# One number read back by VectorE after every step of a four-way scan

## The chip, the cores and the metric

The kernel runs on one core of one Trainium2 chip. The metric is the device time of one execution in microseconds (us). The time before the change is 9154.29 us, the median of three runs (9152.1 to 9154.33).

## What is computed

The input is a float32 image stack of shape (4, 48, 256, 256). Four layers follow each other, each of the form `x = x + f(group_norm(x))`. Layer 0 is a channel attention, layer 1 a gated convolution. Layers 2 and 3, which the change concerns, are the same chain of four scans with different weights:

```
step(carry, inp) = inp + conv1d(carry, w, b)      # 5 taps, 48 channels to 48
down : over the rows, first to last               # input x
up   : over the rows of the result, last to first # the down weights again
right: over the columns, first to last            # the right weights
left : over the columns of that, last to first    # the left weights
```

Every step needs the whole result of the step before it. The four images are independent of each other.

## The kernel before

**Pairs and chains.** The images are worked on two at a time. A pair lies on 96 partitions (48 channels times two neighbouring positions of a row), so that one step of a scan is, for each image of the pair, three matrix products of a 96x96 weight with a 96x128 slice of the last state, summed in PSUM. `scans` (line 965) makes one generator per pair, `chain(pair)` (line 1015); every `yield` in it is one step. I call them chain 0 and chain 1. At the end of `scans` the two are woven: chain 0 takes `lead` = 992 steps alone, then both step in turn, and when chain 0 is through, chain 1 has its last steps alone (lines 1390 to 1404). Beside these last steps `to_rows(0)` rearranges chain 0's result, with copies on GpSimd (line 1383) and ScalarE (line 1385) into a tile `oo`, loaded from `oi`.

**One step** is `step(layer, way, inp, after)`, line 1037. The state lives in four buffers `carry` (`NC` = 4, line 1001) that are used in turn. For each of the two images i:

- TensorE: three matmuls of line 1045 into `ps` (the profile shows six instructions for them, each 96x96 with 96x128);
- VectorE: one addition `carry = ps + inp` (line 1049 for inputs that lie in blocks, line 1053 for plain ones);
- `after(new, b)`, called `keep`: ScalarE writes the new state with its bias to where it is stored (line 1127 down, 1168 up, 1187 for the last row, 1248 right), or, in the left scan, GpSimd adds it to the residual tile `stage` (line 1289) or into `done` (line 1293; this is the last scan of chain 1, the case `direct`).

The addition of step t+1 writes the buffer that was written at step t-3. So besides the sum in `ps` it waits for the `keep` of step t-3, which reads that buffer: for ScalarE in the first three scans, for GpSimd in the left one. In the right scan it also waits for its input: `fetch` (line 1221) copies a strided column out of a block to a plain tile `pre` on GpSimd (line 1225), three steps ahead of its use.

**Order of the work.** Each engine works through one queue in order. The order in the queues is not the order of the Python code: the framework's planner walks through the traced instructions and gives an engine an instruction when, by its own estimates of durations, its inputs are ready; of several that are ready the one that comes first in the code goes first. Line 1317, the `bn_stats` of the first of the two layers, shows it: the code has one of them after each step (`late.pop(0)()`, line 1300), while the trace has eight within four steps. The planner also writes all semaphore waits.

**Stages and transfers.** Down and up work in blocks of 32 rows (line 1117, 1145): down loads the next block (line 1120) and normalises it on ScalarE in place in four pieces (line 1123, `norm`, line 1104, 96x2048 elements each) during the second half of the present one. Right and left work in blocks of 16 columns (lines 1230, 1272) and load the next block at the first step of the present one (lines 1235, 1279, 1280). Stores leave at the ends of blocks (lines 1136, 1201, 1260, 1303, 1311). All of these transfers are issued from SyncE's queue.

Of the kernel before, what the change touches and what calls it, by code (L numbers as in the profile page):

```python
# [9 lines left out]
F32 = mybir.dt.float32  # L10
# [9 lines left out]
P = 96  # L20
# [5 lines left out]
NK = W // (2 * KC)  # L26
# [938 lines left out]
def scans(ctx, tc, xs, out, wts, biases, dram, k, coefs, lead, spare):  # L965
# [13 lines left out]
    nc = tc.nc  # L979
# [8 lines left out]
    wp = pool("c_w", 1)  # L988
# [10 lines left out]
    CB = 2 * KC  # L999
# [15 lines left out]
    def chain(pair):  # L1015
# [4 lines left out]
            nc.gpsimd.memset(c, 0.0)  # L1020
        last = wp.tile([P, 2, W // 2], F32, tag=f"last{pair}", name=f"last{pair}")
        at = [0]

        def slot(name):
            return take(pair, f"{name}{pair}")
# [43 lines left out]
        def load_rows(layer, n, ts, k0, k1):  # L1069

            for r in range(2):
                v = rows_view(ts[r])
                for q in range(2):
                    for b in range(2):
                        nc.sync.dma_start(
                            v[q * C : (q + 1) * C, b, k0:k1].rearrange("c k h w -> c k (h w)"),
                            xs[layer][pair][
                                r * C : (r + 1) * C, b, 2 * k0 + q : 2 * k1 - 1 + q : 2, n * NH : (n + 1) * NH, :
                            ].rearrange("c k h w -> c k (h w)"),
                        )  # L1080

        def layer_of(layer, first):
# [32 lines left out]
            for n in range(NT):  # L1115
                ahead_ = None
                for r in range(RT):
                    if r == 0 and n + 1 < NT:
                        ahead_ = [slot("dn"), slot("dn")]
                        load_rows(layer, n + 1, ahead_, 0, NK)  # L1120
                    if ahead_ and r >= RT // 2 and r % 4 == 0:
                        i = (r - RT // 2) // 4
                        norm(ahead_, i // 2, i % 2)
                    inp = row(now, r)

                    def keep(new, b):
                        nc.scalar.activation(inp[:, b], blocks(new[:, b]), AF.Identity, bias=bias[:, 0:1])  # L1127

                    if n == 0 and r == 0:
                        keep(inner(), slice(0, 2))  # L1130
                    else:
                        step(layer, 0, inp, keep)
                    yield
                if ahead_:
                    for r in range(2):
                        nc.sync.dma_start(D[n][r], now[r])
                    now = ahead_
# [4 lines left out]
            column = None  # L1142
            for n in reversed(range(NT)):
                ahead_ = None
                for r in reversed(range(RT)):
                    if r == RT - 1 and n > 0:
                        ahead_ = [slot("up"), slot("up")]
                        for i in range(2):
                            nc.sync.dma_start(ahead_[i], D[n - 1][i])
                    if n == 0 and r == RT // 4:  # L1150

                        column = slot("col")
                        v = cols_view(column)
                        for par in range(2):
                            for b in range(2):
                                h0 = NH + 1 - par
                                here = slice(par * C, (par + 1) * C)
                                nc.sync.dma_start(
                                    v[here, b, :, h0:, :].rearrange("c q h w -> c q (h w)"),
                                    U[here, b, 0:2, h0:, :].rearrange("c q h w -> c q (h w)"),  # L1160
                                )
                    i = n * RT + r + 1
                    if i == H:
                        continue
                    place = row(now, r)

                    def keep(new, b):
                        nc.scalar.activation(place[:, b], blocks(new[:, b]), AF.Identity, bias=bias[:, 1:2])  # L1168

                    if i == H - 1:  # L1170
                        keep(inner(), slice(0, 2))
                    else:
                        step(layer, 0, place, keep)
                    yield
                    if n == 0 and r < 2:

                        par, h0 = 1 - r, r
                        v = cols_view(column)
                        for q in range(2):
                            nc.sync.dma_start(  # L1180
                                v[par * C : (par + 1) * C, :, q, h0 : h0 + NH, :].rearrange("c b h w -> c b (h w)"),
                                rows_view(now[r])[q * C : (q + 1) * C, :, 0].rearrange("c b h w -> c b (h w)"),
                            )
                if n == 0:

                    def keep(new, b):
                        nc.scalar.activation(last[:, b], new[:, b], AF.Identity, bias=bias[:, 1:2])

                    step(layer, 0, blocks(last), keep)
                    yield  # L1190
                    for q in range(2):
                        nc.sync.dma_start(cols_view(column)[0:C, :, q, 0, :], last[q * C : (q + 1) * C, :, 0:KC])
                for r in range(2):
                    v = rows_view(now[r])
                    par = 1 - r
                    nh = NH - (r == 1 and n == NT - 1)
                    h0 = n * NH + r
                    for q in range(2):
                        for b in range(2):
                            nc.sync.dma_start(  # L1200
                                U[par * C : (par + 1) * C, b, q::2, h0 : h0 + nh, :].rearrange("c k h w -> c k (h w)"),
                                v[q * C : (q + 1) * C, b, :, :nh, :].rearrange("c k h w -> c k (h w)"),
                            )
                if n == 0:
                    for q in range(2):
                        for b in range(2):
                            nc.sync.dma_start(
                                U[0:C, b, q::2, 0, :],
                                last[q * C : (q + 1) * C, b].rearrange("c (k w) -> c k w", w=KC),
                            )  # L1210
                now = ahead_
# [7 lines left out]
            fetched = {}  # L1219

            def fetch(block, n, w):
# [3 lines left out]
                nc.gpsimd.tensor_copy(t, cols_view(block)[:, :, w % 2, :, w // 2])  # L1225
                fetched[g] = t

            for w in range(1, 3):
                fetch(column, 0, w)
            for n in range(NK):  # L1230
                ahead_ = None
                for w in range(CB):
                    if w == 0 and n + 1 < NK:
                        ahead_ = slot("col")
                        nc.sync.dma_start(by_batch(ahead_), block_of(U, n + 1))
                    if w == 0 and n + 1 == NK:
                        stage = slot("stage")
                        nc.sync.dma_start(by_batch(stage), block_of(x, n))
                    if w == 0:
                        lines = slot("lines")  # L1240
                    if w + 3 < CB:
                        fetch(column, n, w + 3)
                    elif ahead_ is not None:
                        fetch(ahead_, n + 1, w + 3 - CB)
                    line = lines_view(lines)[:, w]

                    def keep(new, b):
                        nc.scalar.activation(line[:, b], new[:, b], AF.Identity, bias=bias[:, 2:3])  # L1248

                    if n == 0 and w == 0:  # L1250

                        nc.vector.tensor_scalar(
                            advance(), cols_view(column)[:, :, 0, :, 0], bias[:, 1:2], None, ALU.subtract
                        )
                        keep(inner(), slice(0, 2))
                    else:
                        step(layer, 1, fetched.pop(n * CB + w), keep)
                    yield
                if ahead_ is not None:
                    nc.sync.dma_start(Rt[n], lines)  # L1260
                    column = ahead_
# [3 lines left out]
            if layer == 0:  # L1265
                stats = [wp.tile([P, NK * 4, 6], F32, tag=f"st{pair}{b}", name="st") for b in range(2)]
            following = None


            direct = layer == 1 and pair == NP - 1  # L1270
            done = None
            for n in reversed(range(NK)):
# [3 lines left out]
                for w in reversed(range(CB)):  # L1276
# [18 lines left out]
                    if n == NK - 1 and w == CB - 1:  # L1295
                        keep(inner(), slice(0, 2))
                    else:
                        step(layer, 2, line, keep)
                    if late:
                        late.pop(0)()  # L1300
                    yield
# [227 lines left out]
```

## Time and profile before

| what | value |
|---|---|
| median of the three runs | 9154.29 us |
| the profiled execution | 9152.88 us, of which the span from first to last instruction is 9151.1 us |
| TensorE busy | 8728.1 us, 95% of the span |
| VectorE busy | 3763.0 us, 41%, 10790 instructions |
| ScalarE busy | 3489.5 us, 38% |
| GpSimd busy | 2073.9 us, 23% |
| mean granted TensorE clock | 0.979 |
| first and last matmul of line 1045 | 3234.0 us, 9120.9 us |

A page of this profiler shows busy times by engine and by group of instructions, the idle time before each group and what ended it, and the chain of work that ended last. A row of a group gives line, engine, operation, output and inputs, shapes and count, then busy us and mean ns of one. "PE" is TensorE, "DVE" VectorE, "ACT" ScalarE, "POOL" GpSimd, "SP" SyncE. A "q" behind an engine's name means its sequencer: EVENT_SEMAPHORE is an instruction that only waits. The ends of matmuls are modelled, their starts are recorded.

From the recorded starts of the additions, and the order of the two chains in the program, the scans lie like this in the profiled execution (us from the start):

| chain, layer | down | up | right | left |
|---|---|---|---|---|
| 0, layer 2 | 3243 to 3859 | 3860 to 4202 | 4209 to 4578 | 4579 to 4954 |
| 0, layer 3 | 4987 to 5639 | 5642 to 6306 | 6314 to 6980 | 6985 to 7643 |
| 1, layer 2 | 3542 to 5518 | 5521 to 6188 | 6195 to 6859 | 6863 to 7530 |
| 1, layer 3 | 7567 to 7964 | 7964 to 8310 | 8323 to 8688 | 8689 to 9121 |

Until about 4936 us chain 0 is nearly alone (chain 1 has 63 additions of its own before 4900 us besides 21 at about 3550 us); from 4936 to 7643 us both run; after that chain 1 is alone.

### The profile page before, as it was taken

The numbers are of one execution on the slowest core, as the hardware profiler recorded it, in microseconds if no ns is written. First come the engines' busy times: TensorE is split into PE (matmuls) and PEld (weight loads), VectorE is DVE, ScalarE is ACT, GpSimd is POOL, SyncE is SP. The second block draws the span as 40 slices with busy tenths as digits, with TensorE's granted clock in tenths as the row PEclk, the third lists the DMA queues.
The fourth block names the chain that finished last, engine by engine and source line by source line (L and its number), as shares of the span: only waits on it lengthen the run. The fifth ranks groups of instructions, "written<-read, shape, count | busy, mean of one in ns | idle before, by whom it ended". The sixth has DMA issues, their size and how long they took to land.

```text
span 9151.1 us, 162340 instructions
## 1 busy us (share of the span) xinstructions
PE 8728.1 (95%) x62920; PEld 7283.8 (80%) x62920; DVE 3763.0 (41%) x10790; ACT 3489.5 (38%) x7033; POOL 2073.9 (23%) x3855
## 2 busy tenths in 40 slices
PE   6999999999999887999999999999999999999986
PEld 4777777433333346999999999999999999998986
DVE  3232010234555564444455444444445554343432
ACT  0001000123343356755502766665661006665500
POOL 0000000001111120002464000003446772003464
PEclk9999999999999988999999999999999999999998
DMA  7663323468788868665587773656556787888677
GB/s 149 133 132 87 73 63 72 95 138 175 173 182 181 174 156 178 130 141 138 142 218 172 146 159 92 153 130 169 145 161 186 218 220 158 180 183 203 172 153 146
DMA packets 1177350, 1390.61 MB, mean 152 GB/s; under 512 B 261072, under 2 KB 1103568, under 8 KB 1113600
## 3 DMA queue, kind: packets, MB, share of 16 engines
q1 hardware_dynamic: 1176480, 1379.90, 66.5%
q8 instruction: 493, 8.08, 0.4%
q14 instruction: 281, 2.30, 0.1%
q0 software_dynamic: 96, 0.33, 0.0%
HBM read 812.02 MB, written 509.61 MB: 144 GB/s over the span
## 4 chain that ended last, share of the span: by engine, by line
PE 89%; DMA 4%; DVE 3%; ACT 2%; issue 1%; SPq 1%; POOL 1%; DVEq 0%; POOLq 0%; ACTq 0%
PE ps L1045 58%; PE py L581 7%; PE acc L294 5%; PE acc L295 5%; PE acc L296 4%; PE py L590 4%; PE pt L276 1%; DMA stage<-x 1%; DMA tok<-x 1%; PE ph L698 1%; ACT x1n L541 1%; PE pout L868 1%; PE ptok L751 1%; DMA x<-y 1%; DMA sx<-in_x 1%
## 5 line engine op out<-in xcount | busy, mean ns | idle before, releaser
L1045 PE MATMUL ps<-carry,w 96*96 96x128 f32 x48960 | 5505.8, 275 | 135.9 <-DVE carry L1053 89.3
L1045 PEld LDWEIGHTS ps<-carry,w 96*96 96x96 f32 x48960 | 5456.1, 163 | 188.9 <-DVE carry L1053 100.5
L1225 POOL COPY pre<-col 96x256 f32<-96x256 f32 x1020 | 656.7, 645 | 2737.5 <-DMA col<-last 1948.3
L1248 ACT ACTIVATE lines<-carry,b 96x128 f32<-96x128 f32 (+1 forms) x2044 | 816.9, 402 | 623.6 <-DVE carry L1053 614.5
L1127 ACT ACTIVATE dn<-carry,b 96x128 f32<-96x128 f32 (+1 forms) x2044 | 770.5, 398 | 715.0 <-DVE carry L1049 712.1
L1049 DVE TENSOR_TENSOR carry<-ps,dn 96x128 f32<-96x128 f32 x2280 | 655.2, 288 | 892.9 <-PE ps L1045 803.3
L1053 DVE TENSOR_TENSOR carry<-ps,pre 96x128 f32<-96x128 f32 x2040 | 587.2, 288 | 796.8 <-PE ps L1045 544.0
L1168 ACT ACTIVATE up<-carry,b 96x128 f32<-96x128 f32 x1792 | 718.3, 402 | 481.6 <-DVE carry L1049 480.6
L1053 DVE TENSOR_TENSOR carry<-ps,lines 96x128 f32<-96x128 f32 x2040 | 577.0, 286 | 741.4 <-PE ps L1045 645.4
L1289 POOL TENSOR_TENSOR stage<-stage,carry 96x128 f32<-96x128 f32 (+1 forms) x1533 | 793.1, 521 | 312.3 <-DVE carry L1053 184.2
L1049 DVE TENSOR_TENSOR carry<-ps,up 96x128 f32<-96x128 f32 x1792 | 516.4, 288 | 678.3 <-PE ps L1045 668.9
L581 PE MATMUL py<-x1n,wy 128*96 128x512 f32 x1536 | 700.8, 605 | 30.2 <-ACT x1n L541 27.9
L294 PE MATMUL acc<-xt 128*96 128x288 f32 x2048 | 666.9, 409 | 0.0
L295 PE MATMUL acc<-xs,xt 128*96 128x288 f32 x2048 | 666.9, 407 | 0.0
L581 PEld LDWEIGHTS py<-x1n,wy 128*96 128x96 f32 x1536 | 244.0, 165 | 452.4 <-issue 435.0
L261 ACT ACTIVATE xn<-raw,coef 96x2048 f32<-96x2048 f32 x64 | 133.6, 2094 | 986.9 <-PE pt L276 819.8
L296 PE MATMUL acc<-xt,xs 128*96 128x192 f32 x2048 | 501.7, 327 | 0.0
L279 DVE COPY xt<-pt 128x384 f32<-128x384 f32 x256 | 136.6, 554 | 851.5 <-PE pt L276 650.6
L296 PEld LDWEIGHTS acc<-xt,xs 128*96 128x96 f32 x2048 | 332.2, 165 | 154.4 <-issue 1.5
L295 PEld LDWEIGHTS acc<-xs,xt 128*96 128x96 f32 x2048 | 332.1, 164 | 151.2 <-issue 2.4
L604 DVE TENSOR_TENSOR y<-py,t 96x512 f32<-96x512 f32 x256 | 171.4, 677 | 592.1 <-PE py L590 586.2
L590 PE MATMUL py<-x2n,wy 64*96 64x512 f32 x1536 | 363.0, 601 | 0.0
(179 smaller groups left out, 4843.4 us busy)
## 6 DMA issues: line engine op xcount, KB each, us to landing
stage<-x SPq DMA_DIRECT2D x64, 1536.0 KB
dn<-x SPq DMA_DIRECT2D x240, 384.0 KB
col<-U SPq DMA_DIRECT2D x60, 1536.0 KB
R<-lines SPq DMA_DIRECT2D x60, 1536.0 KB
lines<-R SPq DMA_DIRECT2D x60, 1536.0 KB
D<-dn SPq DMA_DIRECT2D x56, 1536.0 KB
up<-D SPq DMA_DIRECT2D x56, 1536.0 KB
U<-up SPq DMA_DIRECT2D x224, 384.0 KB
```

The source lines that it names most:

```text
L294: nc.tensor.matmul(acc[0], lhsT=xt[:, h + 2, :], rhs=xt[:, here, :], start=first, stop=last)
L295: nc.tensor.matmul(acc[1], lhsT=xt[:, h + 2, :], rhs=xs[:, here, :], start=first, stop=last)
L296: nc.tensor.matmul(acc[2], lhsT=xs[:, h + 2, :], rhs=xt[:, past, :], start=first, stop=last)
L581: nc.tensor.matmul(ps, lhsT=held["w"][0][:, dx], rhs=x1n[:, 2 * c : 2 * c + 2, dx : dx + W], start=dx == 0, stop=False)
L590: nc.tensor.matmul(held["ps"][q + 2 * s], lhsT=held["w"][1][here, dx], rhs=x2n[here, 2 * q : 2 * q + 2, dx : dx + W], start=False, stop=dx ...
L1045: nc.tensor.matmul(ps, lhsT=w_sb[layer][:, way, j, :], rhs=old[:, i, j : j + W // 2], start=j == 0, stop=j == 2)
L1049: nc.vector.tensor_add(new[:, i].rearrange("p (k w) -> p k w", w=KC), ps.rearrange("p (k w) -> p k w", w=KC), inp[:, i])
L1053: nc.vector.tensor_add(new[:, i], ps, inp[:, i])
L1127: nc.scalar.activation(inp[:, b], blocks(new[:, b]), AF.Identity, bias=bias[:, 0:1])
L1168: nc.scalar.activation(place[:, b], blocks(new[:, b]), AF.Identity, bias=bias[:, 1:2])
L1248: nc.scalar.activation(line[:, b], new[:, b], AF.Identity, bias=bias[:, 2:3])
L1289: nc.gpsimd.tensor_add(to[:, b], to[:, b], new[:, b])
```

## The change

A tile `seen` of one number per partition and a list `kept` are added to each chain. After every step, `look` notes the place that this step's `keep` writes for the second image (one column of it). From the fourth call on, VectorE reads the place noted three steps before into `seen`: a copy of 96x1 elements; in the right scan an addition of that number and one number of the next step's fetched column. The list is emptied at the start of every block of 32 rows in down and up, and at the start of right and of left. The additions, `keep` and all else stay as they are; a chain issues 968 readings per layer.

```diff
+        seen = wp.tile([P, 1], F32, tag=f"seen{pair}", name="seen")
+        kept = []
+
+        def look(place, fetched=None):
+            kept.append(place)
+            if len(kept) > 3:
+                if fetched is None:
+                    nc.vector.tensor_copy(seen, kept.pop(0))
+                else:
+                    nc.vector.tensor_add(seen, kept.pop(0), fetched)
...
                         step(layer, 0, inp, keep)
+                    look(inp[:, 1, 0, 0:1])
                     yield
...
                         step(layer, 0, place, keep)
+                    look(place[:, 1, 0, 0:1])
                     yield
...
                         step(layer, 1, fetched.pop(n * CB + w), keep)
+                    if n + 1 < NK or w + 1 < CB:
+                        look(line[:, 1, 0:1], fetched[n * CB + w + 1][:, 1, 0:1])
                     yield
...
                         step(layer, 2, line, keep)
+                    if direct:
+                        look(done[1].rearrange("p (h w) -> p h w", w=2 * CB)[:, 0, n % 2 * CB + w : n % 2 * CB + w + 1])
+                    else:
+                        look(to[:, 1, 0:1])
                     if late:
                         late.pop(0)()
                     yield
```

`kept.clear()` stands at `r == 0` in down, at the start of each block in up, and once ahead of right and of left.

More of the change, by code (lines that the diff above doesn't have):

```diff
@@ L1120, in layer_of @@
                         load_rows(layer, n + 1, ahead_, 0, NK)
+                    if r == 0:
+                        kept.clear()
                     if ahead_ and r >= RT // 2 and r % 4 == 0:
@@ L1144, in layer_of @@
                 ahead_ = None
+                kept.clear()
                 for r in reversed(range(RT)):
@@ L1226, in fetch @@
                 fetched[g] = t
+            kept.clear()
             for w in range(1, 3):
@@ L1267, in layer_of @@
             following = None
+            kept.clear()
             direct = layer == 1 and pair == NP - 1
```

## Prediction

> **What bounds the kernel now.** I read the page's busy times first, then its row of line 1045, then a table of five windows, then the source view of line 1053 and single additions in the timeline.
>
> ```profile
> PE 8728.1 (95%) x62920; PEld 7283.8 (80%) x62920; DVE 3763.0 (41%) x10790; ACT 3489.5 (38%) x7033; POOL 2073.9 (23%) x3855
> ...
> L1045 PE MATMUL ps<-carry,w 96*96 96x128 f32 x48960 | 5505.8, 275 | 135.9 <-DVE carry L1053 89.3
> ```
>
> TensorE is nearly always busy, but its ends are modelled: a short hold of each group does not show as idle. Matmuls counted per window show it:
>
> ```profile
> 3900.00:4150.00 250.00, 250.00 (x2232) 249.72 (x2231) 107.09 (x372) 149.39 (x372) 0.00 (x0) 1.00 0.62 145
> 4350.00:4500.00 150.00, 150.00 (x1312) 146.03 (x1311) 62.91 (x219) 87.59 (x218) 70.27 (x109) 1.00 0.50 136
> 7000.00:7250.00 250.00, 250.00 (x2286) 250.00 (x2285) 132.10 (x429) 0.00 (x0) 196.03 (x381) 1.00 0.78 217
> ```
>
> All three are 100% busy at full clock. With both chains (last row) a matmul comes every 109.3 ns, so 12 of them, one step of a chain, take 1.311 us: TensorE's own rate. Chain 0 alone in up (first row) has 112.0 ns, in right (second) 114.3 ns. The recorded starts of additions give the same: 1.344 us a step alone in down, up and left, 1.3755 us in right. There the loop addition, matmuls, addition is longer than TensorE's work.
>
> ```profile
> L1053 DVEq EVENT_SEMAPHORE  x4051: 21/21/589, 4208.4 to 9121.2; - x193
> ```
>
> There are 4051 instructions that only wait, for the 4080 additions of this line. In the trace's records an addition of down, up or left has an EVENT_SEMAPHORE for TensorE and itself waits for ScalarE or GpSimd; in right the first of two has one for TensorE and ScalarE and waits for GpSimd. From the start of the last matmul to the addition's start (where VectorE was idle over 150 ns) it is 380 ns in the first form, 409 ns in the second, and 310 ns for the 312 additions whose own wait is TensorE. Four of these, then two of right:
>
> ```profile
> 4580.11 0.29 DVE L1053 TENSOR_TENSOR carry<-ps,lines 96x128 f32<-96x128 f32 x1 [0.33 <-PE ps L1045]
> 4580.77 0.29 DVE L1053 TENSOR_TENSOR carry<-ps,lines 96x128 f32<-96x128 f32 x1 [0.37 <-PE ps L1045]
> 4581.43 0.29 DVE L1053 TENSOR_TENSOR carry<-ps,lines 96x128 f32<-96x128 f32 x1 [0.37 <-PE ps L1045]
> 4582.08 0.29 DVE L1053 TENSOR_TENSOR carry<-ps,lines 96x128 f32<-96x128 f32 x1 [0.37 <-PE ps L1045]
> ```
> ```profile
> 4400.12 0.29 DVE L1053 TENSOR_TENSOR carry<-ps,pre 96x128 f32<-96x128 f32 x1 [0.46 <-ACT lines L1248]
> 4400.74 0.29 DVE L1053 TENSOR_TENSOR carry<-ps,pre 96x128 f32<-96x128 f32 x1 [0.34 <-PE ps L1045]
> 4401.49 0.29 DVE L1053 TENSOR_TENSOR carry<-ps,pre 96x128 f32<-96x128 f32 x1 [0.46 <-ACT lines L1248]
> ```
>
> The first set steps by 0.655 us, TensorE's rate, with one chain only; the second by 1.37 us for two. The loop closes: wait form, plus 288 ns addition, plus 131 ns until TensorE streams the dependent group (67 ns to its first start, which then lasts 336 instead of 272), plus 5 x 109 ns to that group's last start. 380+288+131+545 = 1344; 409 gives 1373; 310 gives 1274, below 1311. So **an addition that waits for TensorE alone makes a single chain TensorE-bound**.
>
> **What the Trainium skill says.** "Perfetto Trace Analysis", Identifying Dependency Chains: an instruction that waits on several engines may get EventSemaphore instructions ahead of it; the trace agrees (4051 above). The same page, Tensor Engine Instruction: VectorE, ScalarE and GpSimd are strict FIFO; the trace has VectorE's records in one order, so what stands behind a waiting reading waits too. "SBUF — State Buffer", Who interferes with whom: a VectorE instruction with two SBUF inputs contends with a GpSimd one that reads SBUF, one with a single input outside two-port modes does not. Line 92 (96x1, two inputs) took 155 ns, but 515 ns under a GpSimd copy; the copy of line 1097 (96x1) took 140 ns, begun while GpSimd worked.
>
> **The change part by part.** *Waits removed.* The reading takes over the wait for `keep` of step t-3, and in right that for the fetch. Single-chain steps in the steady rhythm, counted from the trace: right 252+244 = 496, at 1375.5-1311 = 64 ns: 32 us. Down and up 205+237+187+229 = 858, of which 29 in 32 have a reading ahead of them (the list is emptied every block): 778 x 33 ns = 26 us. With both chains nothing is gained, TensorE sets 1.311 already. **Gain 58 us** outside left.
>
> *Readings added.* 4 x 968 = 3872: 2864 copies at 141 ns (line 1097) and 1008 additions at 155 ns (line 92), 560 us of VectorE. An addition ends 0.37 us before the next may start, so one reading fits, if what it reads is there. A follower starts about 80 ns before the reported end of the one ahead (bn_stats, then addition), so a reading costs the queue some 70 ns.
>
> *Where they stand.* The queue's order is the planner's. The bn_stats of line 1317 shows what it does with a ready VectorE instruction: it is put right behind the GpSimd addition that completes its data, ahead of the next scan addition, and waits there.
>
> ```profile
> 4762.34 0.52 POOL L1289 TENSOR_TENSOR stage<-stage,carry 96x128 f32<-96x128 f32 x1 [0.17 <-DVE carry L1053]
> 4762.89 0.69 DVE L1317 BATCH_NORM_STATS2 st<-stage 96x6 f32<-96x512 f32 x1 [0.63 <-POOL stage L1289]
> ```
>
> The reading of step t is ready as soon as `keep` of step t-3 is done. I expect it there, over two steps ahead of its place in the code. In left that is bn_stats's place. Take E as the end of a step's second addition: GpSimd starts at E+78 ns, takes 520, releases at +34, the reading costs 70: the next first addition starts at E+0.70 us instead of E+0.44. Over two steps, because each half passes to the other: 1143 (group start to addition end) + 700 + 288 + 131 + 655 (half a step's matmuls) = 2917, so 1.459 us a step, 115 ns more than now. For ScalarE `keep` ends at E+0.44; SyncE's stores of `keep`'s results stand in the program behind the next step's first addition, so I put the readings of down, up and right there. They are then free in the steady rhythm: ScalarE released at E+0.47, the fetch at E+0.82, the second addition due at E+1.02.
>
> *Costs in left, chain alone.* Chain 0: 157 steps x 115 = 18 us, and some 4 us in its bn_stats steps, where VectorE is full (70 ns x 55). Chain 1: half the blocks end in a wait for `stage` that absorbs them; 7 x 16 x 115 = 13 us. Together 35.
>
> *Slack lost.* Four state buffers let VectorE run up to four steps past a late `keep`. A reading right behind `keep` allows one.
>
> ```profile
> POOL done L1293 <- DMA stage<-x: 105.6, 7, 15.9
> ...
> DVE carry L1053 <- POOL done L1293: 84.6, 22, 11.7
> ```
>
> In chain 1's last left scan GpSimd waits 15 us for `stage` seven times and TensorE only about 11. One step of slack in place of four: 3.3 us more each, 23 us. In down, each `norm` (2.08 us, 52 of them with a chain alone) holds ScalarE; the slack hides it today. The planner allows for a delay, but not exactly; I bound one at 0 and 0.65 us (a group) and take 0.3: 15 us. In chain 1's right scan the 12 strided copies of line 1383 (1.13 us each) delay fetches: 12 x 0.4, and two waits of GpSimd for `col` or `oi` at 4 us: 13 us. SyncE's queue and all transfers are unmoved; a tile is released at most three steps later, with two blocks of spare.
>
> **Sum.** 9152.9 - 58 + 35 + 23 + 15 + 13 = 9181 for the profiled execution, 1.4 us above that for the median: **9182 us**. Its own range is 9145 to 9250, from 0 for slack lost to twice the whole cost of 86 us.
>
> **Rivals.** *Faster, 0.22:* the readings lie where the code has them, behind step t, or the planner puts left's behind the next addition. Then slack stays and nothing waits: gain 58, plus 269 left steps x 33 ns = 9: 9152.9-67+1.4 = 9087. It decides if the reading in left has at least one scan addition ahead of it after `keep` was issued; then 0.6 us of GpSimd is covered by 0.66 us of the next half. For it: the 0.37 us of room; against it: the bn_stats lines. *Much slower, 0.18:* ScalarE's readings too stand ahead of the next first addition. Down and up: start E+0.545, 1.381 us, 37 ns more instead of 33 less: +29 us; right waits for the fetch, E+0.885, 1.551: 496 x 176 = +87; with the 86 above: 9355. *No effect, 0.10:* the additions keep a waiting instruction, for VectorE's own earlier write. The trace has 368 with that form and they too start at 310 ns, so this needs gains and losses that cancel: 9154.
>
> **How the numbers follow.** Likeliest case 0.50: of it 0.31 slower, 0.17 the same, 0.02 faster. About 0.2% (18 us) is what a measurement of this kernel tells from no change. With the rivals: faster 0.02+0.22 = 0.24, same 0.17+0.08 = 0.25, slower 0.31+0.18+0.02 = 0.51. The range runs from 9080 (the faster case) to 9260, leaving out the much slower one.
>
> **What would show it.** Right: EVENT_SEMAPHOREs of lines 1049 and 1053 nearly gone; steps alone at 1.31 us in down, up and right, 1.46 in left; VectorE's readings idle on GpSimd by 0.3 us; waits for `stage` reaching TensorE longer than 11 us. Wrong: left at 1.31 too, or right above 1.38.

## The result, and the profile after

The changed kernel takes 9193.81 us (median of five runs, 9188.08 to 9196.89) against 9154.29 us: ratio 1.0042, 95% interval 1.0028 to 1.0057. It is slower by 0.4%, 12 us above the forecast and inside its range. The profiled execution took 9196.22 us, its span is 9193.6 us.

The busy times and the row of TensorE's scan matmuls on the page of the changed kernel (its line 1060 was 1045):

```profile
PE 8777.9 (95%) x62920; PEld 7258.5 (79%) x62920; DVE 4091.8 (45%) x14662; ACT 3481.8 (38%) x7033; POOL 2039.6 (22%) x3855
...
L1060 PE MATMUL ps<-carry,w 96*96 96x128 f32 x48960 | 5552.1, 275 | 130.9 <-DVE carry L1068 80.8
```

VectorE has 3872 instructions more and 329 us more work; these totals say nothing of where the time went. The same three windows as before (columns: width, then busy us and count of PE, PEld, DVE, ACT, POOL):

```profile
3900.00:4150.00 250.00, 250.00 (x2287) 250.00 (x2286) 120.06 (x553) 152.87 (x382) 0.00 (x0) 1.00 0.61 144
4350.00:4500.00 150.00, 150.00 (x1373) 150.00 (x1372) 83.74 (x343) 91.81 (x229) 73.73 (x115) 1.00 0.54 148
7000.00:7250.00 250.00, 246.84 (x2052) 228.42 (x2051) 115.91 (x554) 0.00 (x0) 169.89 (x342) 1.00 0.70 192
```

In up and right a chain alone now has a matmul every 109.3 ns, TensorE's rate (before: 112.0 and 114.3). In the third window, where both chains run and before had 2286 matmuls, there are 2052: one every 121.8 ns. Here the change costs. The waiting instructions of the addition's line 1068 (1053 before, x4051) are nearly gone:

```profile
L1068 DVEq EVENT_SEMAPHORE  x114: 21/21/50, 4196.5 to 9145.5; - x114
```

Three rows of right, single additions and readings on VectorE:

```profile
4401.32 0.29 DVE L1068 TENSOR_TENSOR carry<-ps,pre 96x128 f32<-96x128 f32 x1 [0.36 <-PE ps L1060]
4401.76 0.15 DVE L1037 TENSOR_TENSOR seen<-lines,pre 96x1 f32<-96x1 f32 x1 [0.15 <-POOL pre L1245]
4401.97 0.29 DVE L1068 TENSOR_TENSOR carry<-ps,pre 96x128 f32<-96x128 f32 x1
```

The reading stands behind the first addition of a step; it waits 0.15 us for GpSimd's fetch, and the second addition still starts 0.65 us after the first. Left alone, chain 0:

```profile
4661.61 0.15 DVE L1035 COPY seen<-stage 96x1 f32<-96x1 f32 x1 [0.64 <-POOL stage L1313]
4661.68 0.28 DVE L1068 TENSOR_TENSOR carry<-ps,lines 96x128 f32<-96x128 f32 x1
4662.14 0.29 DVE L1068 TENSOR_TENSOR carry<-ps,lines 96x128 f32<-96x128 f32 x1 [0.18 <-PE ps L1060]
4663.06 0.15 DVE L1035 COPY seen<-stage 96x1 f32<-96x1 f32 x1 [0.64 <-POOL stage L1313]
```

The reading stands right behind the second addition and ahead of the next first one, and VectorE idles 0.64 us until GpSimd's `keep` is done: 1.455 us a step (4661.61 to 4663.06; before it was 1.344). With both chains in left it is the same, but the two additions that follow one reading belong to two chains (VectorE, then GpSimd; x2 joins two instructions):

```profile
7100.61 0.15 DVE L1035 COPY seen<-stage 96x1 f32<-96x1 f32 x1 [0.91 <-POOL stage L1313]
7100.69 0.47 DVE L1068 TENSOR_TENSOR carry<-ps,lines 96x128 f32<-96x128 f32 x2
7102.07 0.15 DVE L1035 COPY seen<-stage 96x1 f32<-96x1 f32 x1 [0.91 <-POOL stage L1313]
```
```profile
7101.04 0.99 POOL L1313 TENSOR_TENSOR stage<-stage,carry 96x128 f32<-96x128 f32 x2 [0.46 <-DVE carry L1068]
```

The loop reads off these rows: first addition at 7100.69, GpSimd starts 0.36 us later, two keeps take 0.99, the reading starts at 7102.07 and the next addition 0.07 after that. That is 1.45 us for two additions, where TensorE needs 1.311 for their matmuls. TensorE, the bound before, now waits for VectorE, which waits for GpSimd.

From the additions' starts, stretch by stretch (us; "forecast" are the terms of the prediction's sum):

| stretch | before | changed | difference | forecast |
|---|---|---|---|---|
| ahead of the scans | 3242.7 | 3249.0 | +6.2 | 0 |
| down and up, chain 0, then 1 | 617.2, 348.6; 397.3, 358.1 | 607.1, 340.6; 388.4, 347.8 | -37.3 | -26 + 15 |
| right, chain 0, then 1 | 370.3; 366.1 | 355.0; 361.5 | -19.8 | -32 + 13 |
| left, chain 0 | 408.3 | 429.1 | +20.8 | +22 |
| both chains, down to right | 1875.7 | 1877.3 | +1.7 | 0 |
| **both chains in left** | **704.3** | **768.7** | **+64.5** | **0** |
| left, chain 1, to the end | 462.5 | 469.0 | +6.5 | +13 + 23 |
| all | 9151.1 | 9193.6 | +42.5 | +28 |

(A stretch runs to the first addition of the next; "both chains in left" from chain 1's first left step to its next down, chain 0 being in right for the first sixth. Rows may be 0.1 off their sums.)

### The profile page after: what moved, and what is told of

The parts are those of the page before. It is cut to its first block, busy times and chain, and to the rows that moved or that the text cites. A ratio compares the mean times of both kernels' runs of the same rounds, so it can differ in the third digit from the quotient of the medians.

```text
span 9193.6 us, 159757 instructions
## 1 busy us (share of the span) xinstructions
PE 8777.9 (95%) x62920; PEld 7258.5 (79%) x62920; DVE 4091.8 (45%) x14662; ACT 3481.8 (38%) x7033; POOL 2039.6 (22%) x3855
## 5 line engine op out<-in xcount | busy, mean ns | idle before, releaser
L1313 POOL TENSOR_TENSOR stage<-stage,carry 96x128 f32<-96x128 f32 (+1 forms) x1533 | 768.3, 519 | 426.4 <-DVE carry L1068 376.5
L1068 DVE TENSOR_TENSOR carry<-ps,lines 96x128 f32<-96x128 f32 x2040 | 538.2, 280 | 173.9 <-PE ps L1060 124.7
```

What stands on the lines that cost most here:

```text
L1068: nc.vector.tensor_add(new[:, i], ps, inp[:, i])
L1313: nc.gpsimd.tensor_add(to[:, b], to[:, b], new[:, b])
```

## The experiments

In all of them "before" is the kernel before, run beside the experiment on its chip.

**No readings in left.** Edit to the changed kernel:

```diff
-                    if direct:
-                        look(done[1]...)
-                    else:
-                        look(to[:, 1, 0:1])
```

> The readings of the left scan are left out, those of down, up and right stay; the computed result is the same. Theory A (a reading of left stands in VectorE's queue right behind GpSimd's keep and ahead of the next scan addition, so VectorE waits for GpSimd; with both chains it also waits for the other chain's keep): all of the time between the kernel before and the changed one that left costs comes back: chain 0's left alone -21 us, the stretch in which both chains are in left -64 us, chain 1's last left -9 us, so about 9100 us, with 1.31 us a step alone in down, up and right and 1.344 in left. Theory B (the 64 us come from transfers that are shifted by the earlier scans, or from the phase of the two chains): only the some 30 us of the stretches alone come back, about 9165 us.

Measured: 9067.3 us, ratio 0.9915 (0.9902 to 0.9929). Chain 0's left is back at 408.8 us, both chains in left at 704.3; theory B falls. It is 33 us below the expectation: 9 of these lie in that chip's run of before (9145.4), the rest is mainly in the last left (chain 1's, the last row of the table), which with its end fell to 439.7 us where the expectation had some 460 (469 less 9). That opened a question of its own (the tile alone, below).

**Readings in left only.** The three other `look` calls are taken out.

> Only the readings of the left scan stay, those of down, up and right are left out; the computed result is the same. Theory A: the loss of left stands alone, 21 + 64 + 9 us on the kernel before, about 9248 us. Theory B: without the shift from the earlier scans the stretch with both chains in left is as before, and the time is about 9185 us.

Measured: 9237.45 us, ratio 1.0103 (1.0088 to 1.0119). Chain 0's left +19.5, both chains in left +63.6, the last left with its end +9.0. Theory A's stretches again, without any of the earlier readings, so theory B falls here too.

**Readings in left held back.** `step` returns its last `ps`, and in left:

```diff
-                        look(to[:, 1, 0:1])
+                        look(to[:, 1, 0:1], ps[:, 0:1])
```

(the `direct` call likewise)

> All readings stay, but in left a reading is an addition of the kept number and one number of the step's own sum in PSUM, so that it can't be placed ahead of the step's second addition; the computed result is the same. Theory A: it no longer waits for GpSimd's latest keep, left alone runs at TensorE's 1.311 us a step, the stretch with both chains in left comes back to 1.311 a step of each chain: -27 -64 -11 us on the changed kernel, about 9092 us. Theory C (the readings cost by themselves: room in VectorE's queue, or GpSimd and VectorE blocking each other in SBUF): as many readings, with two operands now, so 9194 us or more.

Measured: 9084.0 us, ratio 0.9931 (0.9918 to 0.9943). VectorE with both chains in left:

```profile
7100.60 0.29 DVE L1068 TENSOR_TENSOR carry<-ps,lines 96x128 f32<-96x128 f32 x1 [0.37 <-PE ps L1060]
7100.80 0.14 DVE L1037 TENSOR_TENSOR seen<-stage,ps 96x1 f32<-96x1 f32 x1
7101.25 0.29 DVE L1068 TENSOR_TENSOR carry<-ps,lines 96x128 f32<-96x128 f32 x1 [0.31 <-PE ps L1060]
```

As many readings, 0.14 us each, and none waits for GpSimd: the next addition waits for TensorE, and the stretch takes 700.8 us. So the number of readings costs nothing here; their place does. Chain 0's left came to 408.1, not the 402 expected: its steps alone alternate halves of 0.655 and 0.683 us, where I had expected 0.655 throughout.

**Half the readings in left.**

```diff
-            if len(kept) > 3:
+            if every == 2:
+                if len(kept) > 3:
+                    kept.pop(0)
+                    nc.vector.tensor_copy(seen, kept.pop(0))
+            elif len(kept) > 3:
```

(in left `look` is called with `every=2`; those two lines are not shown)

> In left only every second step has a reading, of what was kept two steps ago, which covers two carry buffers; the computed result is the same. Theory A: half of the stalls stay: left alone at 1.31 and 1.46 us in turn, mean 1.385, and in the stretch with both chains 1.45 becomes 1.38 for two additions: -13 -32 -4 us on the changed kernel, about 9145 us. If a stall every other step were hidden by slack: near 9100 us; if the first of the two readings were the one that costs nothing: near 9190 us.

Measured: 9115.36 us, ratio 0.9964 (0.9952 to 0.9977), and neither half came out as expected. With both chains the loss is gone altogether (704.9 us); alone it is all still there (430.7 us). VectorE in left alone:

```profile
4652.66 0.15 DVE L1036 COPY seen<-stage 96x1 f32<-96x1 f32 x1 [0.63 <-POOL stage L1317]
4652.73 0.61 DVE L1072 TENSOR_TENSOR carry<-ps,lines 96x128 f32<-96x128 f32 x2
4653.99 0.29 DVE L1072 TENSOR_TENSOR carry<-ps,lines 96x128 f32<-96x128 f32 x1 [0.65 <-PE ps L1064]
4654.65 0.29 DVE L1072 TENSOR_TENSOR carry<-ps,lines 96x128 f32<-96x128 f32 x1 [0.37 <-PE ps L1064]
4655.57 0.15 DVE L1036 COPY seen<-stage 96x1 f32<-96x1 f32 x1 [0.64 <-POOL stage L1317]
```

Two steps take 2.91 us from reading to reading, as with a reading in each (2 x 1.455). As I read it, alone one stall in two steps already costs 0.29 us on TensorE's 2.622, since nothing else feeds TensorE, and with a stall in each step their halves overlap; with both chains a reading every fourth addition leaves a loop shorter than TensorE's 2.622 us for these four. This reading is not tested by a run of its own. What the run does show is that the cost isn't proportional to the number of stalls, so they must not be added up.

**A shorter keep.**

```diff
-                            nc.gpsimd.tensor_add(to[:, b], to[:, b], new[:, b])
+                            nc.gpsimd.tensor_add(to[:, b, : W // 4], to[:, b, : W // 4], new[:, b, : W // 4])
```

> The changed kernel, but in left GpSimd's keep adds only 64 of the 128 elements to stage (in all left scans but chain 1's last); the residual of the other half is left out. Theory A (the price of left is a loop, addition, two keeps one behind the other, reading, next addition: 0.36 + 0.47 + 0.52 + 0.10 = 1.455 us for two additions, above TensorE's 1.311): with a keep of some 0.3 us the loop is about 1.0 us and TensorE sets the pace again: about 64 us of the stretch with both chains in left and 22 us of chain 0's left alone come back, about 9108 us. Theory C (a reading costs VectorE's queue its own time, whatever it waits for): 9194 us as the changed kernel.

Measured: 9117.28 us, ratio 0.9965 (0.9952 to 0.9978). A keep of 64 elements takes 353 ns, not 300 (519 with 128). Both chains in left 708.1 us: 61 of the 64 us are back, so the duration of GpSimd's instruction is in the loop and theory C falls. Chain 0's left is at 423.3, only 6 of 21 back: 0.08 + 0.35 + 0.03 + 0.07 us after an addition's end is still later than the 0.37 at which TensorE alone would let the next one start.

**Right with a plain copy.** `look(line[:, 1, 0:1])`, no fetched column.

> The changed kernel, but in right the reading is a copy of the kept number alone, without the fetched column; the computed result is the same. The first addition of a right step then waits for TensorE and for GpSimd's fetch again. If the wait form sets the step as the prediction has it (380 ns with one waiting instruction ahead): 1.344 us a step alone, right of chain 0 loses about 8 us on the changed kernel; right of chain 1 loses 8 and regains about 11 that late fetches cost the reading, so near 9191 us. If it is the 409 ns form: 1.375, both lose 16: about 9215 us. If the second operand bought nothing: 9194 us with 1.311 in right.

Measured: 9197.45 us, ratio 1.0054 (1.0037 to 1.0071). 243 and 242 of the steps alone take 1.34 us; from the last matmul's start to such an addition's start it is 379 ns in 931 cases. So the loop of the prediction holds for a third form: 380 + 288 + 131 + 545 = 1344. Right of chain 0 takes 365.7 us (355.0 in the changed kernel), of chain 1 358.8 (361.5).

**Farther back.** Six carry buffers, reading of five steps ago:

```diff
-    NC = 4
+    NC = 6
...
-            if len(kept) > 3:
+            if len(kept) > 5:
```

> The changed kernel with six carry buffers in place of four, and the reading takes what was kept five steps ago; the computed result is the same. Theory A (the planner puts a reading right behind the keep that completes its data, wherever the code has it): nothing changes, 9194 us, with the 21 and 64 us of left still lost. Rival (the distance in the code, or the slack of the buffers, counts): the loss of left goes, about 9100 us.

Measured: 9326.8 us, ratio 1.0195 (1.018 to 1.021), 133 us above the expectation of theory A. In left theory A holds: chain 0 +22.3, both +62.7. The distance in the code does nothing for a reading that the planner puts right behind its data. But right, of which I had expected nothing, lost 40 us (chain 0), some 18 (both chains) and 50 (chain 1) on the kernel before:

```profile
4351.40 0.15 DVE L1037 TENSOR_TENSOR seen<-lines,pre 96x1 f32<-96x1 f32 x1 [0.80 <-POOL pre L1245]
4351.48 0.28 DVE L1068 TENSOR_TENSOR carry<-ps,pre 96x128 f32<-96x128 f32 x1
4352.02 0.29 DVE L1068 TENSOR_TENSOR carry<-ps,pre 96x128 f32<-96x128 f32 x1 [0.27 <-PE ps L1060]
4353.11 0.15 DVE L1037 TENSOR_TENSOR seen<-lines,pre 96x1 f32<-96x1 f32 x1 [0.80 <-POOL pre L1245]
```

The number kept five steps ago has long been written, so the fetch alone decides when the reading is ready, and the planner puts it ahead of the first addition. This is the place of the prediction's "much slower" rival: it gave right 1.551 us a step; the steps here are 1.71 and 1.38 in turn, mean 1.55. The mean is the rival's; that the steps alternate is in none of its terms.

**The kernel before once more.**

> The kernel before once more, for a second profile: how far the stretch ahead of the scans (3243 us) and chain 1's last left scan (432 us, with waits for transfers) differ from one execution to the next. If both are fixed by the program, they repeat within 3 us; if the transfers vary, by 10 us or more, and differences of that size in these two stretches say nothing on the change.

Measured: 9155.48 us (9148.45 the median on that chip). Every scan stretch repeats within 3 us but the last left with its end, 459.1 us against 462.5; ahead of the scans it is +6.6. So the +6.2 there says nothing on the change, while the some 20 us that the first experiment gained in the last left are more than such a difference.

**The tile alone.** To the kernel before:

```diff
+        seen = wp.tile([P, 1], F32, tag=f"seen{pair}", name="seen")
+        nc.gpsimd.memset(seen, 0.0)
```

> The kernel before with the tile seen of each chain added, set to zero once and never used: no reading at all, but every tile placed after it in SBUF moves by 32 or 64 bytes. In all kernels so far that have this tile, chain 1's last left scan waits some 20 us less for transfers than in the two profiles of before, also with no reading in left (411 us against 432 and 429). If the shifted places (or the planner's answer to them) do that: last left near 411 us here too, the rest as before, about 15 to 20 us below before in all. If the readings of the earlier scans do it, by a shift in time: last left at 430 us and no difference to before.

Measured: 9128.37 us, ratio 0.9973 (0.9963 to 0.9984). The last left with its end takes 444.1 us, 18.4 less, everything else as before within 2 us. The change thus has an effect of its own that isn't a reading at all. The two small tiles push all that lies behind them in SBUF on by 64 bytes: chain 1's five block tiles, but also two of chain 0's five. These seven go from 64 bytes past a multiple of 128 onto a multiple; chain 0's other three stay 32 past one. Chain 0's five matter here because chain 1's last left takes them in turn as `done`, two for each two blocks.

**The tile of 64 bytes.** The same with `[P, 16]`.

> The kernel before with the tile seen of each chain sixteen numbers wide (64 bytes), set to zero once and never used: the tiles of chain 1's blocks move by 128 bytes in place of the 64 of the last run. In the kernel before they begin 64 bytes past a multiple of 128, after the 64-byte shift on a multiple, here 64 past it again. If the place within 128 bytes sets what the transfers of the last left scan take: as before, last left at 429 to 432 us and the whole like before. If it was another effect of an added tile (the planner's order, the memset): near 412 us, some 20 us below before.

Measured: 9149.72 us, ratio 1.0000 (0.9992 to 1.0009); last left with its end 462.3. The seven tiles move by 128 bytes here and the gain is gone, so it isn't the added tile as such. Nor is it the order of the work: in the traces of before, of the 4-byte and of the 64-byte tile every engine has the same operations in the same order, but for the two that set the new tiles to zero. The place within 128 bytes it is.

**No readings in left, all blocks on 128 bytes.**

```diff
+    for at, n in ((first_w, 24), (wp, 8)):
+        nc.gpsimd.memset(at.tile([P, n], F32, tag="pad", name="pad"), 0.0)
```

> The kernel without readings in left, with two padding tiles (96 bytes and 32 bytes, set to zero) so that the block tiles of both chains begin on multiples of 128 bytes; in the run without readings in left three of chain 0's five begin 32 bytes past one, and these take part as done in chain 1's last left. If the place within 128 bytes counts for these too: last left falls further below 411 us, by up to 20 us, and the whole to about 9050 us. If only chain 1's tiles matter: 9067 us again, ratio 0.9915 to the kernel before.

Measured: 9037.36 us, ratio 0.9877 (0.9862 to 0.9893), the fastest of all. The last left with its end takes 413.7 us, 26.0 less than in the first experiment; what the edit moves onto a multiple of 128 bytes are the other three of chain 0's five tiles. GpSimd's waits for `stage` in the last left, kernel before with the 64-byte tile, with the 4-byte tile, and this one (us in total, times, longest; 83.3 in total in the first experiment):

```profile
POOL done L1295 <- DMA stage<-x: 105.6, 7, 15.4
```
```profile
POOL done L1295 <- DMA stage<-x: 88.1, 7, 15.7
```
```profile
POOL done L1319 <- DMA stage<-x: 61.8, 7, 9.1
```

The issue of the `out` stores, with which SyncE is busy ahead of the loads of `stage` (ns, smallest, median, largest), same order:

```profile
L1312 SPq DMA_DIRECT2D out<-done x32: 582/6254/8117, 8722.7 to 9128.2; - x32
```
```profile
L1312 SPq DMA_DIRECT2D out<-done x32: 582/5692/8070, 8727.6 to 9117.1; - x32
```
```profile
L1336 SPq DMA_DIRECT2D out<-done x32: 583/5160/6098, 8673.4 to 9032.6; - x32
```

These stores leave in eight sets of four, from two `done` tiles each. Three sets of the run with the 4-byte tile (start, and us that the four issues take together); in this order both, none and one of the two tiles lie on a multiple of 128 bytes:

```profile
8727.61 17.05 SPq L1312 DMA_DIRECT2D out<-done  x4
8778.44 22.37 SPq L1312 DMA_DIRECT2D out<-done  x4
8834.37 20.21 SPq L1312 DMA_DIRECT2D out<-done  x4
```

The eight: 17.05 and 17.21 us with both on a multiple, 19.21 to 20.21 with one, 21.64 to 22.37 with none. With the 64-byte tile, where none lies on one, all eight take 20.9 to 22.1; with all five on one, 17.0 to 17.3. So it is the stores from chain 0's tiles that get faster. The load of `stage` stands behind a set in SyncE's queue, and so comes sooner: with the 4-byte tile the blocks of the scan that wait for it are 4.2 us shorter than with the 64-byte tile behind each set with two such tiles, 2.6 and 4.4 behind those with one, and differ by -0.8 and +1.2 behind those with none, which is no more than between the two profiles of the kernel before (up to 1.7). For these last two only chain 1's own tiles had moved; no gain shows from that.

**The changed kernel with the tile of 64 bytes**, so that all these tiles lie, within 128 bytes, as before.

> The changed kernel with the tile seen sixteen numbers wide (64 bytes), of which one is used: chain 1's block tiles lie, within 128 bytes, as in the kernel before, so the readings are all that is left of the change. If their own price and the 64-byte shift simply add up: about 20 us above the changed kernel, 9214 us, ratio near 1.0065 to the kernel before, with last left near 455 to 460 us. If in the changed kernel the readings of the last left scan had hidden the waits for transfers anyway: 9194 us, ratio 1.0042.

Measured: 9211.73 us, ratio 1.0067 (1.0053 to 1.0080). Last left with its end 487.9 us, +25.4 on before. The two effects add: 1.0067 x 0.9973 = 1.0040, against 1.0042 measured for the change. The readings alone thus cost 60 us (9211.73 against 9151.45), about twice the +28 of the forecast.

## Why the prediction was right, point by point

The sign, the range and, outside one stretch, the mechanism held. That the sum came out near (+28 for +42.5) is luck, because errors on both sides met: a stretch put at nothing cost 64.5 us, while down and up gained more than forecast, part of the costs did not come, and the place of the new tiles, which is no term of the sum, gave 19 us back.

- **Waits removed: right, term mis-sized.** An addition that waits for TensorE alone starts 310 ns after the last matmul's start, and a chain alone steps at 1.31 us in down, up and right. Down and up gained 37.3 us, where the sum had 26 less 15 for `norm`. The step count was low: all 858 steady steps x 33 ns are 28 us already (in up of chain 0 only 7 steps of 254 still take 1.36 us); the other 9 us I have not traced to single steps. The 15 us for `norm` did not appear: down gained 10.2 and 8.9, up 7.9 and 10.3.
- **Right: right.** Forecast 32 - 13 = 19, measured 15.2 + 4.6. The readings stand where I put them (behind the first addition), and chain 1's right, beside `to_rows`, gave back the difference.
- **Left alone: right.** 1.455 us for 1.459, +20.8 us for +22. The place, right behind `keep` and ahead of the next addition, is the one that the `bn_stats` rows showed. The idle time named as a sign, 0.3 us before a reading, is 0.64; the forecast's own 78 + 520 + 34 ns give 0.63.
- **"With both chains nothing is gained": the step that failed.** It is true of down, up and right (+1.7 us). But the cost was then counted under "Costs in left, chain alone" only, as if TensorE's 1.311 us covered a stall whenever both chains run. In left it doesn't: the queue is shared, so a reading of one chain holds the other chain's addition too, and the loop addition, two keeps, reading takes 1.45 us for two additions. +64.5 us, more than the whole change. All numbers for it were there: 0.36 us to GpSimd's start and two keeps of 0.52.
- **Slack lost, last left: not shown, mis-sized and masked.** Against the kernel of the same placement (the two runs with a 64-byte tile) the last left costs 25.6 us, not 36: its nine blocks without a wait take 23.4 in place of 21.5 us (the first, a step shorter, 22.0 in place of 20.1), 16.7 together; the seven others, the end included, 9.0 more, where I had 13 for stalls and 23 for slack in all. The sign for lost slack did not come: TensorE's longest wait there is 8.4 us, where it had 10.6 and I had named more than 11. So no run shows that any of the 9.0 is lost slack. On top of it the two tiles' 64 bytes moved two of the five tiles that serve as `done` onto multiples of 128 bytes and gave back 18.9. That "all transfers are unmoved" was true of their order, not of their speed.
- **The range of the likeliest case: its ends don't follow from its terms.** With nothing for slack (23 + 15 + 13) the sum is 9131, with the whole cost doubled 9268; it has 9145 and 9250.

- **The rivals.** "No effect" is out: the waiting instructions went. The "faster" rival's place, behind the next addition, is what the held-back run made of left: 9084 us, where the rival had 9087. That these two are so close is luck in part: some 17 us of that run's gain are in the last left (445.4 us for 462.5), most of it from the place of the tiles, which the rival did not have. The "much slower" one came true in the farther-back run's right scan alone.

That the two readings of one kernel can lie in different places (harmless in right, costly in left) is shown by the rows above and by the held-back and the farther-back runs. That the planner's rule is "ready first" is inferred from these places, not shown by itself.

## What to carry to other kernels

In these runs an instruction added only to collect a wait went where its data was ready, not where the code has it. Tie such a one to something that comes late enough (here one number of the step's own sum), or leave it out where the producer is slow. When several chains share a queue, compare the whole loop through the engines with the bound's own time, and don't add up stalls. Before reading a small difference, run the change's tiles without its instructions: placement alone moved this kernel by 0.27%.

## What I had not expected of the hardware

The start of a tile within 128 bytes of SBUF set what stores of short rows out of it cost. The stores from `done` have rows of 32 numbers, 128 bytes; nearly all packets under 512 bytes in the last left are theirs (6144 rows for each of 32 stores, 196608 of 197568 packets in the run with the 4-byte tile). With none, two and five of the five `done` tiles on a multiple of 128 bytes the last left scan (with its end) takes 462, 444 and 414 us (the last without readings in left, which with two takes 440), and the waits for `stage` go 105.6, 88.1 and 61.8 us. That is about 9 us for each tile in both steps.

The Trainium skill, "DMA: Bandwidth & Descriptors", How a descriptor splits into AXI transactions, says that a descriptor which doesn't begin on a 256-byte boundary fetches from the boundary below it; if each row is one descriptor, a row of 128 bytes stays inside one such piece if it begins on a multiple of 128, and half of the rows straddle two if not. The placements agree with that: the two `done` tiles of the 4-byte run begin on multiples of 256, the five of the fastest run 128 past one, and a set of four stores takes 17 us from both. No run here shows the transactions themselves.
